# VectorE's 1x1 run in column tiles, the cosine transform on 32x32 tiles, its loads in three slots, and the gathered pixels stored by half steps

## The chip, the cores and the metric

One Trainium2 chip, one core. The metric is device time in microseconds for one launch. Engines are named as in the profile: PE is TensorE's matmul, PEld its weight load, DVE is VectorE, ACT is ScalarE, POOL is GpSimd, SP is SyncE. POOL and SP here mostly issue DMA transfers.

## What is computed

The input x is 8 images of 32 channels and 128 x 128 pixels in float32. Group normalisation is followed by a block matching that picks, for every pixel, the K = 8 best of 25 shifts in a 5 x 5 window and gathers the 32 channels at those shifts, so there are CK = 256 channels. These go two ways, cut here to the lines that matter:

```
xb = _patch_match_stack(x)                     # [8, 256, 128, 128]
dct = _conv(xb, dct_w, groups=C)               # 8 -> 8 channels in each of 32 groups
h = relu(_conv(_conv(xb, w1), w2, groups=CK, pad=1))   # 1x1, then depthwise 3x3
h = relu(_conv(_conv(h, w3), w4, groups=CK, pad=1))
wiener = sigmoid(_conv(_conv(h, w5), w6, groups=CK, pad=1))
filt = _conv(wiener * dct, inv_dct_w, groups=C)
x = x + _conv(filt, agg_w)                     # layer 0
x = x + 5x5 convolution of the normalised x    # layer 1
```

## The kernel before

**Steps and slots.** An image is worked in steps of R = 8 rows, 16 steps and one more that finishes the last rows (NS + 1 = 17 for each image, 136 in all). Each step of the main loop has four slots, in the order i = 3, 2, 1, 0. Slots 3, 2 and 1 each run one of the three pairs "1x1, then depthwise 3x3", each for an earlier step than the one before it in the chain; slot 0 finishes the step that is two behind: it multiplies the sigmoid by the cosine transform and applies the last 1x1. Every slot also gathers one quarter of a step's pixels for the steps to come (`gather_load` three quarters ahead, `gather_select` one ahead, `gather_pixels` now).

**The 1x1 is split over two engines' depthwise convolutions.** `pointwise_t` (matmul line L694, tile p) makes output channels 0 to 127 for a depthwise convolution on PE (`depthwise_t`, L750, tile pw). `pointwise_v` (L670, tile pv) makes output channels 128 to 255 for a depthwise convolution on DVE (`depthwise_v`, L724). `pointwise_t` and `depthwise_t` use weight tiles 32 columns wide, four side by side, each writing 32 partitions of the output. `pointwise_v` uses one weight tile of 128 x 128: for each half step of 4 rows, two matmuls of 512 elements that add up. A float32 matmul shows in the trace as two matmul records.

**The cosine transform.** `gather_pixels` (L632, tile pg) fills xb, which `pointwise_v` and `pointwise_t` read, and which is stored to a DRAM tensor xbd once for each step (L641, one transfer of 1 MB). Since the transform is needed much later than the 1x1, `final_load` loads the 8 rows again from xbd as xf (L790, eight transfers of 128 KB, issued together at the end of slot 0). xf has one buffer. `final_dct` (L809, tile pc) multiplies xf by ldct on four 64 x 64 tiles of the array, two banks of PSUM at a time, and DVE multiplies the result into acc (L817). `final_add` (L830, tile pa) follows in the next slot; DVE adds its result to the input (L838).

**Order.** PE, DVE and ACT run their instructions in the order in which the program writes them. Between these fixed pieces small background tasks are let in from queues: D (DVE, rationed by `tick`), A (ACT), P and Q (PE). They make the next image's costs and the layer 1 of the image before (`layer1`, its matmul is L923 with 64 x 64 tiles, from queue P). POOL's and SP's orders are left to a list scheduler, by program order and readiness. Tiles pv, p, pg, pc, pa and L923's p share a PSUM pool ps_x of five banks. Transfers issued by POOL use eight semaphores in turn, so one waits until the eighth before it has landed.

Of the kernel before, what the change touches and what calls it, by code (L numbers as in the profile page):

```python
# [8 lines left out]
F32 = mybir.dt.float32  # L9
# [6 lines left out]
P = 128  # L16
C, K, H, W = 32, 8, 128, 128
CK = C * K
# [25 lines left out]
def bm3d_conv_preact(  # L44
# [58 lines left out]
    lw5 = const.tile([P, 2, CK], F32, name="lw5")  # L103


    ldct = const.tile([P, 2, 64], F32, name="ldct")
    lagg = const.tile([P, 2, C], F32, name="lagg")


# [90 lines left out]

    queues = {"D": deque(), "A": deque(), "P": deque(), "Q": deque()}

    PAIR = 1.95
    pairs = [0]
# [90 lines left out]

    def mixes():

        dq = work.tile([P, 2, K], F32, name="dq", tag="dq", bufs=1)  # L300
        src = dct_w.rearrange("(m h c i) k a b -> m h k c (i a b)", m=2, h=2, i=K)
        for k in range(K):
            for m in range(2):
                for h in range(2):
                    p = 64 * h + 8 * k
                    nc.sync.dma_start(dq[p : p + 8, m], src[m, (h + m + 1) % 2, k])
        m8 = work.tile([P, 8], F32, name="m8", tag="m16", bufs=1)
        yield "D", 1.0, 10
        nc.vector.tensor_reduce(
            m8,  # L310
            cst[:, C_M32 : C_M32 + C].rearrange("p (a c) -> p c a", c=8),
            axis=mybir.AxisListType.X,
            op=ALU.add,
        )
        for m in range(2):
            nc.vector.tensor_tensor(
                ldct[:, m].rearrange("p (c i) -> p c i", i=K),
                m8.unsqueeze(2).to_broadcast([P, 8, K]),
                dq[:, m].unsqueeze(1).to_broadcast([P, 8, K]),
                ALU.mult,  # L320
            )

        iv = work.tile([P, 2, K], F32, name="iv", tag="iv", bufs=1)
        nc.sync.dma_start(iv, inv_w.rearrange("(m p) k a b -> p m (k a b)", p=P))
        ag = work.tile([C, CK], F32, name="ag", tag="xr")
        nc.sync.dma_start(ag, agg_w.rearrange("c i a b -> c (i a b)"))
        for m in range(2):
            yield "D", 0.5
            ib = work.tile([P, P], F32, name=f"ib_{m}", tag="xm")
            nc.vector.tensor_tensor(  # L330
                ib.rearrange("p (c k) -> p c k", k=K),
                cst[:, C_M16 : C_M16 + 16].unsqueeze(2).to_broadcast([P, 16, K]),
                iv[:, m].unsqueeze(1).to_broadcast([P, 16, K]),
                ALU.mult,
            )
            yield "P", 0
            ps = ps_x.tile([P, 512], F32, name=f"ps_ag_{m}", tag="x")[:, :C]
            nc.tensor.transpose(ps, ag[:, m * P : (m + 1) * P], ident[:C, :C])
            agt = work.tile([P, C], F32, name=f"agt_{m}", tag="agt")
            nc.scalar.copy(agt, ps)  # L340
            yield "P", 0
            ps2 = ps_x.tile([P, 512], F32, name=f"ps_ia_{m}", tag="x")[:, :C]
            nc.tensor.matmul(ps2, ib, agt, start=True, stop=True)
            nc.scalar.copy(lagg[:, m], ps2)
# [276 lines left out]
    def gather_pixels(b, s4, f):  # L621

        n, h = s4 // 2, s4 % 2
        if h == 0 and f == 0:
            xbs[b, n] = xbp.tile([P, 2, R, W], F32, name=f"xb_{b}_{n}", tag="xb")
        xb, xt = xbs[b, n], xts[b, s4]
        sels = [selss.pop((b, s4, f, k2)) for k2 in range(2)]
        pg = ps_x.tile([P, 2, 4, HW], F32, name=f"pg_{b}_{s4}_{f}", tag="x")
        for t in range(NT // 2):
            xa, xz = TW * t, min(TW * (t + 1), HW)  # L630
            for j in range(4):
                nc.tensor.matmul(  # L632
                    pg[C * j : C * (j + 1), :, :, xa:xz],
                    xt[: 8 * QW, f * (NT // 2) + t],
                    sels[j // 2][: 8 * QW, :, j % 2, :, xa:xz],
                    start=True,
                    stop=True,
                )
        nc.scalar.copy(xb[:, :, 4 * h : 4 * h + 4, HW * f : HW * (f + 1)], pg)
        if h == 1 and f == 1:  # L640
            nc.gpsimd.dma_start(xbd[b][:, :, R * n : R * (n + 1)], xb)  # L641

# [15 lines left out]
    def pointwise_v(i, b, n, lhsT, src):  # L660

        v = tv[i - 1]
        if n == NS:
            nc.gpsimd.memset(v[:, i + 1 : 6], 0.0)
        r0, r1 = (i - 1 if n == 0 else 0), (R if n < NS else i - 1)
        for h in range(0, r1, 4):
            hr = min(4, r1 - h)
            ps = ps_x.tile([P, 4, W], F32, name=f"pv{i}_{b}_{n}_{h}", tag="x")
            for g in range(2):
                nc.tensor.matmul(  # L670
                    ps[:, :hr],
                    lhsT[:, g, P:CK],
                    src(g)[:, h : h + hr],
                    start=g == 0,
                    stop=g == 1,
                )
            a = max(h, r0)
            nc.scalar.copy(v[:, 2 + a : 2 + h + hr, 1 : 1 + W], ps[:, a - h : hr])  # L678

# [89 lines left out]
    def final_load(b, n):  # L769
        j0, j1 = (3, R) if n == 0 else (0, R if n < NS else 3)  # L770
        ya, yz = R * n - 3 + j0, R * n - 3 + j1

        whole = j1 - j0 == R
        nr, nw = (2, W) if whole else (j1 - j0, C)
        xr = work.tile([P, 2 * W], F32, name=f"xr_{b}_{n}", tag="xr")
        xr = xr[:, : nr * nw].rearrange("p (r w) -> p r w", w=nw)
        for j in range(4):
            ra = ya + 2 * j if whole else ya
            xa = 0 if whole else C * j
            nc.gpsimd.dma_start(  # L780
                xr[C * j : C * (j + 1)], x[b, :, ra : ra + nr, xa : xa + nw]
            )

        xf = xbp.tile([P, 2, R, W], F32, name=f"xf_{b}_{n}", tag="xf", bufs=1)
        src = xbd[b].rearrange("(j m h c) g y x -> g m h j c y x", j=4, m=2, h=2)
        for m in range(2):
            for h in range(2):
                for g in range(2):
                    p = 64 * h + C * g
                    nc.gpsimd.dma_start(  # L790
                        xf[p : p + C, m, j0:j1], src[g, m, (h + m + 1) % 2, :, :, ya:yz]
                    )
        return xr, xf, j0, j1

    def final_dct(b, n, acc, xf, j0, j1):

        for r0 in range(0, R, 4):
            a, z = max(r0, j0), min(r0 + 4, j1)
            if a >= z:
                continue  # L800


            pc = [
                ps_x.tile([P, 4, W], F32, name=f"pc_{b}_{n}_{m}_{r0}", tag="x") for m in range(2)
            ]
            for h in range(2):
                for m in range(2):
                    o = 64 * ((h + m + 1) % 2)
                    nc.tensor.matmul(  # L809
                        pc[m][o : o + 64, : z - a],  # L810
                        ldct[64 * h : 64 * h + 64, m],
                        xf[64 * h : 64 * h + 64, m, a:z],
                        start=True,
                        stop=True,
                    )
            for m in range(2):
                nc.vector.tensor_mul(acc[m][:, a:z], acc[m][:, a:z], pc[m][:, : z - a])  # L817

    def final_add(b, n, acc, xr, j0, j1):

# [26 lines left out]
    def layer1(b):  # L847
# [60 lines left out]
        for c in range(0, C, 8):  # L908
            if c == 0 or not last:
                yield "D", 2.0, 1 if last else 3  # L910
                normalise(c)
            yield "P", 0
            ps = [
                ps_x.tile([P, 4, W], F32, name=f"p5_{b}_{c}_{e}", tag="x") for e in range(2)
            ]
# [107 lines left out]
    def turn(credit):  # L1023
        now[0] += 1
        run("D", credit)
        run("A")
        run("P")
        run("Q")

    def until(cond, credit):  # L1030
# [3 lines left out]
    with tc.manual_schedule(engines=ORDERED):  # L1034
        push(prep(0))
        push(weights())
        push(mixes())
        xbd[0] = dram.tile([P, 2, H, W], F32, name="xbd_0", tag="xbd")
        for i in range(3):
            nc.gpsimd.memset(tb[i][0:64, :, 0], 0.0)  # L1040
        for u in range(7):
# [12 lines left out]
        for s in range(len(steps) + 2):  # L1054
            if s < len(steps):
                b, n = steps[s]
                if s == 2:
                    push(bands())
                if n == (0 if b else 4) and b + 1 < NB:
                    until(lambda: b in ready, 4.0)  # L1060
                    push(prep(b + 1))
                if n == NS - 1 and b + 1 < NB:
                    until(lambda: b + 1 in ready, 4.0)
                    xbd[b + 1] = dram.tile([P, 2, H, W], F32, name=f"xbd_{b+1}", tag="xbd")
            for i in (3, 2, 1, 0):
                si = s - (i - 1 if i else 2)
                live = 0 <= si < len(steps)
# [15 lines left out]
                run("P")  # L1083
                if live and not i:
                    final_dct(bi, ni, accs[3, bi, ni], xf, j0, j1)

                run("Q")
                if s < len(steps):
# [18 lines left out]
                if live and not i:  # L1107
                    later = end(bi, ni, xr, j0, j1)
                if not i and 0 <= s - 1 < len(steps):
                    fins[s - 1] = final_load(*steps[s - 1])  # L1110
        next(kept, None)
        for _ in later:
            pass
# [63 lines left out]
```

## Time and profile before

| | us |
|---|---|
| median of three runs | 6739.54 |
| lowest, highest | 6728.39, 6740.50 |
| the profiled execution | 6733.76 |
| its span, first to last instruction | 6732.0 |

Busy shares of the span: PE 94%, DVE 87%, ACT 75%, POOL 53%; the mean granted TensorE clock is 0.979. A busy PE is not a PE at its peak: the ends of matmuls are modelled, and overlapping matmuls are merged. How densely PE really works is read from the distance between the starts of consecutive groups of matmuls. In the rows of the timeline, "x8" is the number of records, and the bracket at a line's end is idle time and what ended it.

### The profile page before, as it was taken

Reading aid. Unit: us, or ns where it says so; the run is one execution under the profiler, and the core shown is the slowest. Engines: PE = TensorE matmul, PEld = TensorE weight load, DVE = VectorE, ACT = ScalarE, POOL = GpSimd, SP = SyncE. Lnnn points to the kernel's source line nnn. Section 1 sums busy time; section 2 is a strip of 40 time slices with the busy share of each in tenths; the row PEclk is TensorE's granted clock in tenths of the full one; section 3 lists DMA queues with packets and bytes.
Section 4 is the critical chain, followed back from the end, with each engine's and each line's share of the span. In section 5 each row is a group of like instructions: output and inputs, shape, how many; then the busy total and the mean of one; then the engine's idle time right before and its main releaser. Section 6 shows DMA issues by size and latency. Waiting matters only on the chain. (4 is left out here: it accounts for less than half of the span.)

```text
span 6732.0 us, 216242 instructions
## 1 busy us (share of the span) xinstructions
PE 6334.0 (94%) x92898; PEld 3283.2 (49%) x92898; DVE 5863.1 (87%) x8826; ACT 5060.0 (75%) x6698; POOL 3535.4 (53%) x5527
## 2 busy tenths in 40 slices
PE   5898899999999999999999999999999999999997
PEld 1454455454555545554554545545445454454553
DVE  7889988999889998898988998899888889877776
ACT  5787778777687777877777776877768777687772
POOL 8355447544475454654546544565446654344334
PEclk8899999999999999999999999999999999999998
DMA  4666666766666675666756657566665666566663
GB/s 95 148 151 154 146 153 149 166 154 158 153 158 157 149 166 139 165 155 155 173 129 166 163 144 167 144 167 159 148 155 146 165 151 154 141 164 166 157 150 83
DMA packets 811645, 1020.36 MB, mean 152 GB/s; under 512 B 257072, under 2 KB 622192, under 8 KB 810688
## 3 DMA queue, kind: packets, MB, share of 16 engines
q0 software_dynamic: 424608, 747.17, 44.3%
q1 hardware_dynamic: 383568, 258.11, 17.8%
q8 instruction: 732, 11.99, 0.8%
q10 hardware_dynamic: 2512, 1.25, 0.1%
q14 instruction: 225, 1.84, 0.1%
HBM read 554.82 MB, written 217.54 MB: 115 GB/s over the span
## 5 line engine op out<-in xcount | busy, mean ns | idle before, releaser
L724 DVE SCALAR_TENSOR_TENSOR acc<-tv,dwv,acc 128x1024 f32<-128x1024 f32 (+3 forms) x3264 | 4032.2, 1237 | 256.0 <-ACT acc L721 148.2
L750 PE MATMUL pw<-t,dwd 96*32 96x254 f32 (+7 forms) x31680 | 2127.8, 421 | 74.8 <-DMA t<-t 52.2
L603 POOL DMA_DIRECT2D ib<-idxd x1024 | 749.5, 733 | 1615.0 <-ACT sel L618 1352.0
L750 PEld LDWEIGHTS pw<-t,dwd 96*32 96x32 f32 (+1 forms) x31680 | 1056.9, 111 | 936.0 <-issue 442.8
L617 ACT ACTIVATE ib<-ib,nplace 128x1024 bf16<-128x1024 bf16 x1024 | 1170.6, 1143 | 50.4 <-DMA ib<-idxd 50.4
L618 ACT ACTIVATE sel<-ib 128x1024 f32<-128x1024 bf16 x1024 | 1085.8, 1060 | 32.6
L694 PE MATMUL p<-acc,lw 128*32 128x256 f32 x16768 | 998.3, 383 | 22.8 <-ACT tv L678 22.8
L670 PE MATMUL pv<-acc,lw 128*128 128x512 f32 (+1 forms) x2112 | 970.5, 601 | 29.9 <-DVE acc L817 24.2
L790 POOL DMA_DIRECT2D xf<-xbd x1088 | 650.9, 629 | 282.6 <-DMA out_dram<-xy 82.3
L694 PEld LDWEIGHTS p<-acc,lw 128*32 128x32 f32 x16768 | 558.5, 111 | 454.4 <-ACT tv L678 57.8
L450 ACT ACTIVATE df<-df 128x786 f32<-128x786 f32 (+2 forms) x576 | 467.6, 860 | 331.3 <-DVE df L442 328.6
L678 ACT COPY tv<-pv 128x512 f32<-128x512 f32 (+2 forms) x784 | 436.6, 578 | 370.0 <-PE pv L670 364.6
L632 PE MATMUL pg<-sel,xt 120*32 120x88 f32 (+1 forms) x24576 | 612.7, 244 | 62.1 <-ACT sel L618 46.6
L632 PEld LDWEIGHTS pg<-sel,xt 120*32 120x32 f32 x24576 | 553.1, 111 | 235.1 <-ACT sel L618 60.5
L670 PEld LDWEIGHTS pv<-acc,lw 128*128 128x128 f32 x2112 | 378.9, 191 | 480.6 <-issue 384.3
L442 DVE TENSOR_TENSOR df<-xn 128x786 f32<-128x786 f32 (+2 forms) x576 | 531.8, 974 | 83.3 <-PE pd L457 82.3
L763 ACT ACTIVATE acc<-pw 128x512 f32<-128x512 f32 (+2 forms) x808 | 440.4, 573 | 197.8 <-PE pw L750 195.6
L728 ACT ACTIVATE acc<-acc 128x1024 f32<-128x1024 f32 (+3 forms) x408 | 417.3, 1023 | 225.1 <-DVE acc L724 224.9
L701 ACT COPY t<-p 128x512 f32<-128x512 f32 x800 | 424.2, 570 | 119.0 <-PE p L694 116.9
L721 ACT ACTIVATE acc<-tv,dwv 128x1024 f32<-128x1024 f32 (+3 forms) x408 | 454.8, 1115 | 50.6 <-PE pa L830 33.7
L670 PE MATMUL pv<-xb,lw 128*128 128x512 f32 x1024 | 474.8, 606 | 0.0
L694 PE MATMUL p<-xb,lw 128*32 128x256 f32 x8192 | 467.5, 380 | 0.0
(155 smaller groups left out, 5911.1 us busy)
## 6 DMA issues: line engine op xcount, KB each, us to landing
ib<-idxd POOLq DMA_DIRECT2D x1024, 256.0 KB, 4.7
xbd<-xb POOLq DMA_DIRECT2D x128, 1024.0 KB, 6.9
xf<-xbd POOLq DMA_DIRECT2D x960, 128.0 KB, 7.2
t<-t SPq DMA_DIRECT2D x792, 128.0 KB
t<-t SPq DMA_DIRECT2D x384, 256.0 KB
tv<-tv SPq DMA_DIRECT2D x384, 130.0 KB
xt<-xtd POOLq DMA_DIRECT2D x240, 180.0 KB, 4.7
xtd<-xl POOLq DMA_DIRECT2D x192, 96.0 KB, 3.0
```

The source lines that it names most:

```text
L442: nc.vector.tensor_sub(df[:, :, ca:cz], xn[:, r0 : r0 + SR, ca:cz], xn[:, r0 + dy : r0 + dy + SR, ca + dx : cz + dx],)
L450: nc.scalar.activation(df[:, :, ca:cz], df[:, :, ca:cz], AF.Square)
L603: nc.gpsimd.dma_start(ib.rearrange("p g k y x -> p g (k y x)"), idxd[b][s4 % 8 // 2, s4 // 8 * 2 + s4 % 2, f] .rearrange("(g e k) x -> e g ...
L617: nc.scalar.activation(ib, ib, AF.Square, bias=nplace)
L618: nc.scalar.activation(sel, ib, AF.Relu, scale=-1.0, bias=1.0)
L632: nc.tensor.matmul(pg[C * j : C * (j + 1), :, :, xa:xz], xt[: 8 * QW, f * (NT // 2) + t], sels[j // 2][: 8 * QW, :, j % 2, :, xa:xz], star ...
L670: nc.tensor.matmul(ps[:, :hr], lhsT[:, g, P:CK], src(g)[:, h : h + hr], start=g == 0, stop=g == 1,)
L694: nc.tensor.matmul(ps[C * r : C * (r + 1), e, :nb], lhsT[:, g, s], rows[:, r : r + 4 * nb - 3 : 4], start=g == 0, stop=g == 1,)
L721: nc.scalar.activation(acc, rows, AF.Copy, scale=tap)
L724: nc.vector.scalar_tensor_tensor(acc, rows, tap, acc, op0=ALU.mult, op1=ALU.add)
L750: nc.tensor.matmul(pt[u][C * j : C * (j + 1), ka:kz, :nb, xa:xz], dwd[0:hi, i - 1, u, j, dx + 1], t[0:hi, j, ka:kz, :nb, xa + dx : xz + dx ...
L790: nc.gpsimd.dma_start(xf[p : p + C, m, j0:j1], src[g, m, (h + m + 1) % 2, :, :, ya:yz])
```

## The change

Four parts.

1. `pointwise_v` issues four matmuls of 32 output columns (j = 0 to 3) in place of one of 128. The result and the number of streamed elements for each tile are the same.
2. `final_dct` works on 32 x 32 tiles. For each s of four (which half of the channels, which 4 rows) four tiles on a diagonal of the array write the four quadrants of one PSUM bank: sixteen tiles and four banks in all. ldct, its loads (64 small transfers in place of 32) and xf's channel order are changed to fit.
3. `final_load` becomes a generator that issues the loads of xf in four pieces: s = 0 at the end of slot 0, s = 1 at the end of slot 3, s = 2 and 3 at the end of slot 2. Each piece has one transfer, or two where the partitions wrap around. xbd's layout becomes [256, 128, 128], and the store is made for each half step, in four transfers of 32 partitions.
4. layer 1's matmuls get a queue L of their own, run in slots 3, 2 and 1 and not in slot 0.

```diff
-        if h == 1 and f == 1:
-            nc.gpsimd.dma_start(xbd[b][:, :, R * n : R * (n + 1)], xb)
+        if f == 1:
+            for j in range(4):
+                nc.gpsimd.dma_start(
+                    xbd[b].rearrange("(c g j) y x -> j c g y x", g=2, j=4)[
+                        j, :, :, 4 * s4 : 4 * s4 + 4
+                    ],
+                    xb[C * j : C * (j + 1), :, 4 * h : 4 * h + 4],
+                )
...
             for g in range(2):
-                nc.tensor.matmul(
-                    ps[:, :hr],
-                    lhsT[:, g, P:CK],
-                    src(g)[:, h : h + hr],
-                    start=g == 0,
-                    stop=g == 1,
-                )
+                for j in range(4):
+                    nc.tensor.matmul(
+                        ps[C * j : C * (j + 1), :hr],
+                        lhsT[:, g, P + C * j : P + C * (j + 1)],
+                        src(g)[:, h : h + hr],
+                        start=g == 0,
+                        stop=g == 1,
+                    )
...
-        src = xbd[b].rearrange("(j m h c) g y x -> g m h j c y x", j=4, m=2, h=2)
-        for m in range(2):
-            for h in range(2):
-                for g in range(2):
-                    p = 64 * h + C * g
+        yield xr, xf, j0, j1
+        src = xbd[b].rearrange("(m p) y x -> m p y x", m=2)
+        for s in range(4):
+            if s:
+                yield
+            m, r0 = s // 2, s % 2 * 4
+            a, z = max(r0, j0), min(r0 + 4, j1)
+            for pa, pz, at in ((0, P - C * s, C * s), (P - C * s, P, 0)):
+                if a < z and pa < pz:
                     nc.gpsimd.dma_start(
-                        xf[p : p + C, m, j0:j1], src[g, m, (h + m + 1) % 2, :, :, ya:yz]
+                        xf[pa:pz, m, a:z],
+                        src[m, at : at + pz - pa, R * n - 3 + a : R * n - 3 + z],
                     )
...
+        parts = [(s, max(s % 2 * 4, j0), min(s % 2 * 4 + 4, j1)) for s in range(4)]
+        parts = [(s, a, z) for s, a, z in parts if a < z]
+        pc = {
+            s: ps_x.tile([P, 4, W], F32, name=f"pc_{b}_{n}_{s}", tag="x") for s, a, z in parts
+        }
+        for s, a, z in parts:
+            for q in range(4):
+                o = C * ((q + s) % 4)
+                nc.tensor.matmul(
+                    pc[s][o : o + C, : z - a],
+                    ldct[C * q : C * (q + 1), s],
+                    xf[C * q : C * (q + 1), s // 2, a:z],
+                    start=True,
+                    stop=True,
+                )
+        for s, a, z in parts:
+            m = s // 2
+            nc.vector.tensor_mul(acc[m][:, a:z], acc[m][:, a:z], pc[s][:, : z - a])
...
-            yield "P", 0
+            yield "L", 0
...
                 if live and not i:
                     final_dct(bi, ni, accs[3, bi, ni], xf, j0, j1)
+                else:
+                    run("L")
...
                 if not i and 0 <= s - 1 < len(steps):
-                    fins[s - 1] = final_load(*steps[s - 1])
+                    loads = final_load(*steps[s - 1])
+                    fins[s - 1] = next(loads)
+                if 0 <= s - (1 if not i else 2) < len(steps):
+                    for _ in range({0: 1, 3: 1, 2: 2, 1: 0}[i]):
+                        next(loads)
```

More of the change, by code (lines that the diff above doesn't have):

```diff
@@ L103, in bm3d_conv_preact @@
     lw5 = const.tile([P, 2, CK], F32, name="lw5")
-    ldct = const.tile([P, 2, 64], F32, name="ldct")
+    ldct = const.tile([P, 4, C], F32, name="ldct")
     lagg = const.tile([P, 2, C], F32, name="lagg")
@@ L197, in bm3d_conv_preact @@
     xtd, xbd, idxd, x1d, stats = {}, {}, {}, {}, {}
-    queues = {"D": deque(), "A": deque(), "P": deque(), "Q": deque()}
+    queues = {"D": deque(), "A": deque(), "P": deque(), "L": deque(), "Q": deque()}
     PAIR = 1.95
@@ L298, in mixes @@
     def mixes():
-        dq = work.tile([P, 2, K], F32, name="dq", tag="dq", bufs=1)
-        src = dct_w.rearrange("(m h c i) k a b -> m h k c (i a b)", m=2, h=2, i=K)
-        for k in range(K):
-            for m in range(2):
-                for h in range(2):
-                    p = 64 * h + 8 * k
-                    nc.sync.dma_start(dq[p : p + 8, m], src[m, (h + m + 1) % 2, k])
-        m8 = work.tile([P, 8], F32, name="m8", tag="m16", bufs=1)
+        dq = work.tile([P, 4, K], F32, name="dq", tag="dq", bufs=1)
+        src = dct_w.rearrange("(m q c i) k a b -> m q c k (i a b)", m=2, q=4, i=K)
+        for s in range(4):
+            for q in range(4):
+                for c in range(4):
+                    p = C * q + K * c
+                    nc.sync.dma_start(dq[p : p + K, s], src[s // 2, (q + s) % 4, c])
+        m4 = work.tile([P, 4], F32, name="m4", tag="m16", bufs=1)
         yield "D", 1.0, 10
         nc.vector.tensor_reduce(
-            m8,
-            cst[:, C_M32 : C_M32 + C].rearrange("p (a c) -> p c a", c=8),
+            m4,
+            cst[:, C_M32 : C_M32 + C].rearrange("p (a c) -> p a c", a=4),
             axis=mybir.AxisListType.X,
@@ L314, in mixes @@
         )
-        for m in range(2):
+        for s in range(4):
             nc.vector.tensor_tensor(
-                ldct[:, m].rearrange("p (c i) -> p c i", i=K),
-                m8.unsqueeze(2).to_broadcast([P, 8, K]),
-                dq[:, m].unsqueeze(1).to_broadcast([P, 8, K]),
+                ldct[:, s].rearrange("p (c i) -> p c i", i=K),
+                m4.unsqueeze(2).to_broadcast([P, 4, K]),
+                dq[:, s].unsqueeze(1).to_broadcast([P, 4, K]),
                 ALU.mult,
@@ L784, in final_load @@
         xf = xbp.tile([P, 2, R, W], F32, name=f"xf_{b}_{n}", tag="xf", bufs=1)
-        src = xbd[b].rearrange("(j m h c) g y x -> g m h j c y x", j=4, m=2, h=2)
-        for m in range(2):
-            for h in range(2):
-                for g in range(2):
-                    p = 64 * h + C * g
+        yield xr, xf, j0, j1
+        src = xbd[b].rearrange("(m p) y x -> m p y x", m=2)
+        for s in range(4):
+            if s:
[4 more added lines that the diff above has]
+                if a < z and pa < pz:
@@ L790, in final_load @@
                     nc.gpsimd.dma_start(
-                        xf[p : p + C, m, j0:j1], src[g, m, (h + m + 1) % 2, :, :, ya:yz]
+                        xf[pa:pz, m, a:z],
+                        src[m, at : at + pz - pa, R * n - 3 + a : R * n - 3 + z],
                     )
-        return xr, xf, j0, j1
+        yield
     def final_dct(b, n, acc, xf, j0, j1):
[L797 to L817, printed above, removed]
+        parts = [(s, max(s % 2 * 4, j0), min(s % 2 * 4 + 4, j1)) for s in range(4)]
@@ new lines, in final_dct @@
+        parts = [(s, a, z) for s, a, z in parts if a < z]
[3 more added lines that the diff above has]
+        for s, a, z in parts:
+            for q in range(4):
+                o = C * ((q + s) % 4)
[6 more added lines that the diff above has]
+                )
@@ L1037, in bm3d_conv_preact @@
         push(mixes())
-        xbd[0] = dram.tile([P, 2, H, W], F32, name="xbd_0", tag="xbd")
+        xbd[0] = dram.tile([CK, H, W], F32, name="xbd_0", tag="xbd")
         for i in range(3):
@@ L1063, in bm3d_conv_preact @@
                     until(lambda: b + 1 in ready, 4.0)
-                    xbd[b + 1] = dram.tile([P, 2, H, W], F32, name=f"xbd_{b+1}", tag="xbd")
+                    xbd[b + 1] = dram.tile([CK, H, W], F32, name=f"xbd_{b+1}", tag="xbd")
             for i in (3, 2, 1, 0):
@@ L1085, in bm3d_conv_preact @@
                     final_dct(bi, ni, accs[3, bi, ni], xf, j0, j1)
+                else:
+                    run("L")
                 run("Q")
```

## The prediction

> **What bounds the kernel now.** I read the page first, then the stretches of time, the timeline of PE over one step, and the waits. From the page, the engines and the slices:
>
> ```profile
> PE 6334.0 (94%) x92898; PEld 3283.2 (49%) x92898; DVE 5863.1 (87%) x8826; ACT 5060.0 (75%) x6698; POOL 3535.4 (53%) x5527
> ...
> PE   5898899999999999999999999999999999999997
> ...
> DVE  7889988999889998898988998899888889877776
> ```
>
> PE is nearly full, and DVE is not far behind it: two engines, each with the whole image's chain running through it. The stretches (columns: span, then busy PE, PEld, DVE, ACT, POOL) say where which of them leads:
>
> ```profile
> 4200.00:5000.00 800.00, 767.55 (x11433) 400.82 (x11426) 719.48 (x1089) 623.60 (x826) 435.13 (x679) 0.99 0.65 157
> ...
> 5800.00:6400.00 600.00, 592.63 (x9067) 310.93 (x9056) 471.60 (x488) 456.28 (x588) 266.11 (x423) 1.00 0.63 158
> ```
>
> With the next image's costs in the background (first line) PE is at 96% and DVE at 90%. In the last image, which has no next one (second line), PE is at 99%, DVE at 79%: PE alone sets the pace.
>
> How much of a busy PE is work? In the timeline of PE (start, length, group) the distance between starts is what counts:
>
> ```profile
> 3001.69 3.70 PE L670 MATMUL pv<-xb,lw 128*128 128x512 f32 x8
> 3005.32 0.87 PE L457 MATMUL pd<-df,neg 128*32 128x390 f32 x8
> 3006.00 3.64 PE L694 MATMUL p<-xb,lw 128*32 128x256 f32 x64
> 3009.45 1.13 PE L632 MATMUL pg<-sel,xt 120*32 120x88 f32 x48
> 3010.41 5.31 PE L750 MATMUL pw<-t,dwd 96*32 96x512 f32 x48
> 3015.65 1.95 PE L809 MATMUL pc<-xf,ldct 64*64 64x512 f32 x16
> 3017.52 1.15 PE L632 MATMUL pg<-sel,xt 120*32 120x88 f32 x48
> ...
> 3022.96 2.79 PE L750 MATMUL pw<-t,dwd 96*32 96x256 f32 x48 [1.71 <-DMA t<-t]
> ...
> 3067.91 2.97 PE L809 MATMUL pc<-xf,ldct 64*64 64x512 f32 x16
> 3070.81 1.15 PE L632 MATMUL pg<-sel,xt 120*32 120x88 f32 x48
> ```
>
> p: 64 records in 3.45 us, four side by side, so 16 sets of 256 elements at 0.216 us, or 0.43 us for 512. pv: 8 records of 512 in 3.63 us. The weight loads of pv show its pitch:
>
> ```profile
> 3001.69 0.30 PEld L670 LDWEIGHTS pv<-xb,lw 128*128 128x128 f32 x2 [0.41 <-issue]
> 3002.22 0.19 PEld L670 LDWEIGHTS pv<-xb,lw 128*128 128x128 f32 x1 [0.24 <-issue]
> 3002.65 0.19 PEld L670 LDWEIGHTS pv<-xb,lw 128*128 128x128 f32 x1 [0.24 <-issue]
> ```
>
> Also 0.43 for 512. So one wide tile and four narrow ones stream at the same rate, and the split itself buys nothing. What pv has on top are its ends: the first distance is 0.53 (0.10 too long), and 0.09 pass between the end of its eighth (3001.69 + 0.53 + 7 x 0.43 = 3005.23) and the next group. Reading the single starts in the trace, another 0.11 lie between the end of the pw before it and its own start, and 0.03 in the head of the next group: 0.33 to 0.34 us for going into the 128 x 128 arrangement and back. From pd to p, both 32 columns wide, there is nothing (3005.68 + 0.33 for 390 elements is 3006.00).
>
> **The change part by part.**
>
> *pv.* By the order of the matmuls in the trace PE goes 490 times into a stretch of 128 x 128 work; 314 of these hold pv alone, the others also transposes, which keep their switch. Gain on PE: 314 x 0.338 = 106 us. Streaming is unchanged (8 sets of 0.43); the records go from 8 to 32 a call, and p above issues such records without a gap. Layer 1's matmuls (28 stretches) used to follow pv or precede pc in part and now pay both of their own ends, some 8 us. Net 98.
>
> *pc.* Now 1.87 us: 4 sets x 0.43 = 1.72, and 0.15 of ends. After: 32 records of 512. If all sixteen tiles run together that is 2 sets, 0.86, with the ends as before (32 x 32 is again another arrangement) and about 0.1 for issuing twelve more loads before the first set is complete: 1.1 us, a gain of 0.77. There are 2112 / 16 = 132 full steps' worth: 101 us. This is the disputed term. The trace never runs more than four tiles at once. What it shows is that in pc today four tiles (two row tiles x two column tiles) start within 0.02 us of each other and the next four 0.43 later, although both row tiles write the same bank, in different partitions.
>
> The Trainium skill speaks here on both sides. "TensorEngine Tiling (Array Packing)", section Restrictions and Gotchas, says that different row tiles cannot use one PSUM bank at the same time. The new pc puts four row tiles into each bank, so by that rule its sixteen tiles go one at a time within each bank, on the order written four in a row: 8 sets, 3.43 + 0.15 us, 1.7 us worse than now. The row above contradicts the rule for two row tiles in one bank, so I do not follow it. "TensorE: Matmul & The Clock Gate", Part 3 (Measured speedup vs the span model), gives 10.6 times for sixteen tiles, not 16: an estimate from that is 0.86 x 16 / 10.6 = 1.3 us, a gain of about 0.5 instead of 0.77, 66 us instead of 101. I take the trace's 101 and keep 66 as the lower end of the good case; the bounds outside it are 5 sets (if the second pass of one diagonal holds up the next diagonal; 2.15 us, minus 57 us) and 8 sets (minus 226 us).
>
> *DVE* has the same multiplications (four of 128 x 512 a step): nothing. PSUM: pc takes four of five banks as before. Where layer 1 sat directly before pc, pc took 2.90 in place of 1.87 (the last two timeline lines), since two banks were still held; 13 such places, 13 us, go away, but layer 1 comes up elsewhere, where pv or p want those banks. I count it as zero, within plus or minus 13.
>
> *POOL and DMA.* Stores: 8 transfers of about 0.63 us (the mean of today's 128 KB xf issue) for one of 0.73: +4.3 us a step, 128 steps, +551. Loads: 7 for 8 (3 in the last step of an image): 168 fewer, -106. POOL's busy time goes to about 3980, 59%. It is covered by POOL's longest wait, where it stands before ib loads until ACT is done:
>
> ```profile
> POOL ib L603 <- ACT sel L618: 1352.0, 414, 9.3
> ...
> DVE xr L838 <- PE pa L830: 280.0, 68, 10.6
> ...
> PE pw L750 <- DMA t<-t: 52.2, 32, 4.4
> ```
>
> That is 10 us a step against 3.3 added. If that cover were gone, the price would be at most the 3.3 us, in the steps where POOL is late. Behind a waiting store stand the next ib and xf; ib is asked for two slots ahead. Bytes are the same, in pieces of 2 KB for 4 KB; today's packets of 2048 bytes take 0.09 us and those of 4096 0.19, so the DMA engines see no difference. SP: 32 more tiny transfers of dq at 0.72 us, 23 us, at 24 us into the run; SP's first other work is at 204 us. Zero.
>
> *xf's lead.* Today the last xf issue stands 34 us (median; least 7.5) ahead of pc, and a landing takes:
>
> ```profile
> DMA to landing us min/median/max: 2.5/7.0/14.8
> ```
>
> The pieces s = 2 and 3 are now written one slot (about 12 us) before pc. If POOL also issues them there, behind four stores, about 5 us of lead remain for 7 of landing, and PE waits some 2 us a step. The scheduler may issue them earlier, since they are ready once the last pc is done, and the trace shows POOL transfers issued ahead of earlier ones that wait. I take zero; bounds are 0 and +2 x 132 = 264 us.
>
> *What of PE's 199 us reaches the end.* DVE waits for PE (xr for pa) in 68 of 136 steps, by 4 us each: there PE is late, and 1.5 us saved a step are 1.5 us of time. In the other half DVE arrives after PE, and a shorter PE mostly waits longer. In the last image, 17 steps, all counts. So (17 + 119 / 2) / 136 = 56%, plus part of the rest, since the two are only a few us apart: two thirds. A second loss: slot 0 has neither pv nor p, and in 32 steps its pw waits for a t<-t transfer, which a shorter pc doesn't hasten: included. 199 x 2/3 = 133. From the profiled execution's 6733.8: 6601; the median of the runs shown is 5.8 above it, so 6600 to 6606. I say 6600.
>
> **The rivals.**
>
> *Sixteen tiles don't run together* (slower side). At 8 sets pc costs 3.58 us; PE gets +226 - 98 = +128, and work added to the fuller engine counts nearly whole: about 6850. It decides from the point where pc takes more than 1.87 + 98 / 132 = 2.6 us, between 5 and 6 sets. For it: the rule above, and nothing in the trace shows sixteen. Against it: pc's two row tiles in one bank. At 5 sets the kernel would still gain, about 6705. Chance of 6 sets or more 8%, of about 5 sets 5%.
>
> *xf comes late.* +264 on PE against -199: 6750 to 6800. Chance 8%; halfway, near no change, 3%.
>
> *DVE becomes the bound.* DVE's 5863 us don't shrink, and at 6600 it is at 89% overall and 93% where the next image is prepared. If only the last image's 17 steps and a quarter of the rest gain (25 + 45 us): about 6670. For it: 90% against 96%. Against it: of DVE's idle 869 us, 280 are spent on pa. Chance 14%.
>
> *The main case*, 6600 (6525 to 6650): 62%. The upper limit of the gain is all 199 us and some calmer t<-t transfers because of smaller stores: 6520.
>
> **How the numbers follow.** About 0.2%, 13 us, is what a measurement of this kernel can tell from no change. Faster: 62 + 14 + 5 and a part of the halfway case, 81%; within 0.2%: 3%; slower: 8 + 8 = 16%. The range leaves out the slower cases and the best tail: 6520 to 6720.[...]
>
> **What would show it.** Right: pv appears as 128*32 with 32 records a call, its start-to-next is 3.45 where it was 3.63, and the 0.11 before it is gone; pc reads 32*32, x32, with about 1.1 us to the next group; "issue" waits before pv shrink; DVE's wait for pa falls from 280, its wait share elsewhere rises; POOL is near 59%. Wrong: pc above 2.6 us; a wait of pc on a transfer of xf; PE waiting for DVE or ACT more than 100 us longer than before (then DVE is the bound); new waits for ib in ACT (then POOL is).

## The result and the profile after

The changed kernel is no faster, and by a little slower: 6745.13 us (median of 12 runs, 6736.35 to 6756.93) against 6733.99 us (median of 12, 6725.13 to 6742.49) for the kernel before on the same chip. The ratio is 1.0019, with a 95% interval of 1.001 to 1.0028. The forecast was 6600 us, range 6520 to 6720. The profiled execution of the changed kernel has a span of 6735.4 us (before: 6732.0) and a mean granted TensorE clock of 0.969 (before: 0.979).

The page's line of engines, after:

```profile
PE 6200.2 (92%) x104418; PEld 3213.7 (48%) x104418; DVE 5863.8 (87%) x8828; ACT 5056.7 (75%) x6698; POOL 3845.5 (57%) x6255
```

PE is busy for 134 us less than before, in a span that is no shorter: so much has turned into idle time. The two stretches (span, then busy PE, PEld, DVE, ACT, POOL, then clock, DMA share, GB/s) say the same. In the stretch with the next image's preparation PE went from 96% to 94%:

```profile
4200.00:5000.00 800.00, 748.55 (x12668) 381.94 (x12662) 714.22 (x1084) 617.39 (x818) 470.94 (x765) 0.98 0.62 154
5800.00:6400.00 600.00, 587.40 (x10418) 315.17 (x10414) 478.30 (x494) 463.70 (x600) 302.82 (x507) 0.99 0.62 160
```

Where nothing waits, the two edits of PE's work did what they were to do. The timeline of PE after, for a step like the one shown before:

```profile
2993.07 5.36 PE L757 MATMUL pw<-t,dwd 96*32 96x256 f32 x96
2998.23 3.63 PE L677 MATMUL pv<-xb,lw 128*32 128x512 f32 x32
3001.67 0.85 PE L457 MATMUL pd<-df,neg 128*32 128x393 f32 x8
3002.33 3.64 PE L701 MATMUL p<-xb,lw 128*32 128x256 f32 x64
3005.78 1.15 PE L632 MATMUL pg<-sel,xt 120*32 120x88 f32 x48
3006.72 5.33 PE L757 MATMUL pw<-t,dwd 96*32 96x512 f32 x48
3011.98 1.33 PE L817 MATMUL pc<-xf,ldct 32*32 32x512 f32 x32
3013.24 1.16 PE L632 MATMUL pg<-sel,xt 120*32 120x88 f32 x48
```

From pv's start to the next start it is now 3.44 us, eight sets of 0.43 and nothing else; before, it was 3.63. The weight loads of that pv come in fours, 0.43 apart from the first on:

```profile
2998.23 0.14 PEld L677 LDWEIGHTS pv<-xb,lw 128*32 128x32 f32 x4
2998.66 0.14 PEld L677 LDWEIGHTS pv<-xb,lw 128*32 128x32 f32 x4 [0.29 <-issue]
```

The pw ahead of it takes 5.16 us from start to start, and pd behind it 0.66, without the 0.11 and 0.03 that lay there before. pc takes 1.26 us (3011.98 to 3013.24) where it took 1.87: its 32 records do run as two sets of sixteen tiles. Read singly in the trace, the first sixteen start within 0.29 us and the next sixteen begin 0.45 us after the first, so four row tiles in one bank do not hold each other up.

The time went elsewhere. The waits after (us in total, times, longest): POOL's, DVE's and pw's answer to those shown of before, the others are pc's:

```profile
POOL ib L603 <- ACT sel L618: 1256.4, 406, 13.2
DVE xr L847 <- PE pa L839: 275.2, 66, 13.1
PEld pc L817 <- DVE acc L826: 80.5, 12, 7.2
PE pc L817 <- DVE acc L826: 69.6, 12, 6.2
PE pw L757 <- DMA t<-t: 43.9, 21, 5.2
PE pc L817 <- DMA xf<-xbd: 25.0, 7, 6.4
```

DVE's wait for pa, which the prediction took for PE being late, is 275 us where it was 280. And pc waits in twelve places for DVE's multiplication (L826) to free a PSUM bank, 70 us together. One such place, in PE's timeline and then in DVE's (whose first row is cut at the window's edge):

```profile
2921.62 4.48 PE L932 MATMUL p<-xm,band 64*64 64x512 f32 x40
...
2959.68 1.19 PE L817 MATMUL pc<-xf,ldct 32*32 32x512 f32 x24
2966.58 1.93 PE L817 MATMUL pc<-xf,ldct 32*32 32x512 f32 x8 [5.71 <-DVE acc L826]
```

```profile
2948.92 17.01 DVE L731 SCALAR_TENSOR_TENSOR acc<-tv,dwv,acc 128x1024 f32<-128x1024 f32 x13
2965.85 1.87 DVE L826 TENSOR_TENSOR acc<-acc,pc 128x512 f32<-128x512 f32 x3
2968.58 0.69 DVE L826 TENSOR_TENSOR acc<-acc,pc 128x512 f32<-128x512 f32 x1 [0.86 <-PE pc L817]
2969.18 1.28 DVE L944 TENSOR_TENSOR xy<-xy,p 128x512 f32<-128x512 f32 x2
```

Layer 1's matmul (2921.62) fills two of the five banks; DVE empties them at 2969.18, since the addition L944 comes from the rationed background queue. pc comes in between and finds three banks: 24 of its 32 records run, and the last eight wait until DVE is through with its taps (2965.85). In the kernel before, layer 1 held two banks just as often, for 9 to 24 us, but where it met pc it stood directly ahead of it:

```profile
3063.61 4.48 PE L923 MATMUL p<-xm,band 64*64 64x512 f32 x40
```

```profile
3058.07 10.52 DVE L724 SCALAR_TENSOR_TENSOR acc<-tv,dwv,acc 128x1024 f32<-128x1024 f32 x8
```

So pc came 4.3 us later, at 3067.91, when DVE's taps were nearly through (their end: 3068.59), and was done in 2.90 us. The four pieces of layer 1 in each of images 2 to 7, before, hold their banks for 23, 9, 24 and 9 us from the end of their matmuls; after: 23, 44, 9 and 25.

Such a wait is followed by a second loss. The same place in stretches, the granted clock is the third column from the right:

```profile
2950.00:2959.00 9.00, 9.00 (x157) 4.50 (x160) 8.79 (x8) 8.68 (x12) 1.47 (x2) 1.00 0.72 189
2959.00:2966.00 7.00, 1.87 (x32) 0.28 (x24) 6.82 (x7) 2.88 (x4) 1.42 (x2) 0.89 0.41 119
2966.00:2971.00 5.00, 4.42 (x64) 2.31 (x68) 4.09 (x10) 0.56 (x1) 1.93 (x3) 0.50 0.16 42
2971.00:2976.00 5.00, 5.00 (x96) 2.81 (x92) 4.35 (x22) 2.99 (x5) 5.00 (x4) 0.97 0.36 88
```

After the wait PE runs at half its clock: pg takes 1.71 us from start to start (2968.44 to 2970.15) in place of 0.97. Over the whole run the trace grants half clock for 421 us, before for 288. Of PE's waits behind the first 600 us of the changed kernel's trace, all 28 of 4 us or more have half clock beginning in them or within 4 us of their end, and 18 of the 48 of 2 to 4 us have it too.

### The profile page after: what moved, and what is told of

It is laid out like the page before. It is cut to its first block, busy times and chain, and to the rows that moved or that the text cites. A ratio compares the mean times of both kernels' runs of the same rounds, so it can differ in the third digit from the quotient of the medians.

```text
span 6735.4 us, 240331 instructions
## 1 busy us (share of the span) xinstructions
PE 6200.2 (92%) x104418; PEld 3213.7 (48%) x104418; DVE 5863.8 (87%) x8828; ACT 5056.7 (75%) x6698; POOL 3845.5 (57%) x6255
## 5 line engine op out<-in xcount | busy, mean ns | idle before, releaser
L757 PEld LDWEIGHTS pw<-t,dwd 96*32 96x32 f32 (+1 forms) x31680 | 1082.9, 111 | 916.0 <-issue 423.2
L677 PE MATMUL pv<-acc,lw 128*32 128x512 f32 x8448 | 955.0, 589 | 52.5 <-DVE acc L826 39.6
L642 POOL DMA_DIRECT2D xbd<-xb x1024 | 546.1, 569 | 100.1 <-DMA ib<-idxd 33.6
L801 POOL DMA_DIRECT2D xf<-xbd x920 | 494.7, 551 | 177.0 <-PE pc L817 99.7
L677 PEld LDWEIGHTS pv<-acc,lw 128*32 128x32 f32 x8448 | 282.4, 110 | 539.0 <-issue 417.7
L677 PE MATMUL pv<-xb,lw 128*32 128x512 f32 x4096 | 469.9, 593 | 0.0
```

Source lines behind the costliest of these rows:

```text
L642: nc.gpsimd.dma_start(xbd[b].rearrange("(c g j) y x -> j c g y x", g=2, j=4)[j, :, :, 4 * s4 : 4 * s4 + 4], xb[C * j : C * (j + 1), :, 4 * ...
L677: nc.tensor.matmul(ps[C * j : C * (j + 1), :hr], lhsT[:, g, P + C * j : P + C * (j + 1)], src(g)[:, h : h + hr], start=g == 0, stop=g == 1,)
L757: nc.tensor.matmul(pt[u][C * j : C * (j + 1), ka:kz, :nb, xa:xz], dwd[0:hi, i - 1, u, j, dx + 1], t[0:hi, j, ka:kz, :nb, xa + dx : xz + dx ...
L801: nc.gpsimd.dma_start(xf[pa:pz, m, a:z], src[m, at : at + pz - pa, R * n - 3 + a : R * n - 3 + z],)
```

## The experiments

Four theories were set up in turn. A: layer 1's own queue holds PSUM banks over the next pc. B: PE and DVE take turns, and what PE saves becomes a wait for DVE (or for ACT behind DVE). C: POOL has too much to do, and xf comes late. D: as B, but because the background work of DVE is heaped into slot 0. All ratios are to the kernel before on the same chip.

**Layer 1's queue alone, in the kernel before** (before_L), and the changed kernel without it (after_P), cut to the line that differs:

```diff
-            yield "P", 0        # layer1, in the kernel before
+            yield "L", 0        # and run("L") in slots 3, 2, 1
```

> The kernel before with one part of the change alone: layer 1's matmul in the queue L (slots 3, 2 and 1 only). Theory A (banks): the queue moves this matmul from just before pc to a slot from which its two PSUM banks are held over the next pc until DVE's additions, rationed by tick, come; pc then has three of its four banks and stands until DVE has done its eight taps. Two such places an image of about 8 us and one of 9 in the slot before: 7 x 25 = 175 us at most, so 6800 to 6900. Theory B (DVE is the bound, whatever PE saves): no change, 6725 to 6745. Theory C (POOL and the late xf loads take the gain): no change either.

> The changed kernel with layer 1's matmul back in the queue P; all else as changed. Theory A: the 8 us waits of pc for DVE go away but for the places where this matmul stands directly before pc (about 2 us each, two an image); of PE's 199 us two thirds come through: 6610 to 6660, pc waiting for DVE acc under 50 us in all. Theory B: 6730 to 6750. Theory C: 6730 to 6750, with pc waiting for xf as before.

before_L took 6801.12 us, ratio 1.0102 (1.0082 to 1.0123): the queue alone costs about 69 us. Layer 1's banks are now held for 23, 45, 9 and 25 us, and the waits show the same mark (in the kernel before PE has no such wait, and PEld 11.6 us of it, at most 0.9 at a time):

```profile
PEld pc L809 <- DVE acc L817: 66.3, 12, 5.9
PE pc L809 <- DVE acc L817: 55.8, 12, 5.0
```

after_P took 6693.95 us, ratio 0.9942 (0.9923 to 0.9962): without the queue, the rest of the change gains 0.58%, 39 us. With after_P_late below it has the lowest ratio of the kernels that compute everything, though the intervals of before_pv, after_P_once and after_P_even overlap with its own. So A is right about part 4, worth 52 us inside the change (1.0019 - 0.9942 = 0.77%), but falls short of its 6610 to 6660: most of the expected gain is lost in another way.

**Layer 1's additions let in earlier, changed kernel** (after_add). The queue L stays; the addition is taken out of DVE's ration and run in the same slot.

```diff
-            yield "D", 3.6 if last else 1.6
+            if last:
+                yield "D", 3.6
+            else:
+                yield "A", 0
```

> The changed kernel with one edit: DVE's two additions after layer 1's matmul are run in the same slot (queue A) and not when tick's ration allows. The queue L stays. Theory A: both banks are free before the next pc, so the waits of pc for DVE fall to the level of the kernel before and the gain appears: 6590 to 6650. Theory B: 6730 to 6750, since DVE has the same work. Theory C: 6730 to 6750.

It took 6752.44 us, 1.0035 (1.0022 to 1.0049): a miss. The banks come free earlier (held for 9, 15, 16 and 15 us), but the addition now stands in DVE's fixed order behind the taps, and pv is what waits for it:

```profile
PEld pv L677 <- DVE xy L947: 77.9, 15, 8.4
PE pv L677 <- DVE xy L947: 69.2, 14, 8.2
```

**pv's column tiles alone, in the kernel before** (before_pv), the diff's second hunk and nothing else:

> The kernel before with pv in column tiles alone. PE loses 314 switches of 0.338 us, 106 us. Theory A: two thirds of it, 6655 to 6680. Theory B: no change, 6725 to 6745. Theory C: as A, since no transfer is changed.

6694.72 us, 0.9951 (0.9933 to 0.9969): 33 us come out of about 98 that PE saves.

**All pieces of xf at once, at the end of slot 0** (after_P_once, otherwise after_P), and **the store once for each step** (after_P_store1: after_P with four transfers of 256 KB in place of eight of 128 KB):

```diff
-                if 0 <= s - (1 if not i else 2) < len(steps):
-                    for _ in range({0: 1, 3: 1, 2: 2, 1: 0}[i]):
+                    for _ in range(4):
                         next(loads)
```

> The changed kernel with layer 1's matmul in queue P, and all pieces of xf issued at the end of slot 0 again. Once an image, where POOL issues 31 transfers of the next image's xtd in a row, the last piece of xf is now issued 3 us after pc has started (before: 9 us ahead), and pc with the column set after it loses some 8 us. Theory C (late xf): this goes away, 7 x 6 to 8 us less than with the three slots: 0.9942 falls to 0.986 to 0.988 of the kernel before, 6635 to 6650. Theory B (DVE takes up what PE saves): no more than 10 us less, 6680 to 6695, with PE's wait moved on to pv.

> The changed kernel with layer 1's matmul in queue P, and the gathered pixels stored once a step (four transfers of 256 KB) and not by half steps (eight of 128 KB). POOL loses 512 issues of 0.57 us, 290 us of its time. Theory C in the form 'POOL's load costs time': 20 to 40 us less than 6694. Theories A and B: no difference beyond 10 us, since POOL's added work lies in its wait for ACT.

In after_P (33.0 us in all), as in the changed kernel (25.0), a piece of xf comes late for pc about once an image, where POOL is busy with a row of some 30 other transfers (L422). In the changed kernel:

```profile
2804.60 1.09 PE L817 MATMUL pc<-xf,ldct 32*32 32x512 f32 x16
2809.85 4.15 PE L817 MATMUL pc<-xf,ldct 32*32 32x512 f32 x16 [4.16 <-DMA xf<-xbd]
```

after_P_once has no such wait left, and took 6703.91 us, 0.9947 (0.9929 to 0.9964), as much as after_P: C is out as the cause. PE waits in other places instead. One of them is pv, for a bank that DVE's multiplication of pc frees; in the kernel before that wait is 24.2 us. Another is pw, for the transfers t<-t, 52.2 us in the kernel before; whether these come late because of DVE was not followed:

```profile
PE pv L677 <- DVE acc L826: 55.7, 28, 3.2
PE pw L757 <- DMA t<-t: 78.9, 31, 6.4
```

after_P_store1 took 6727.45 us, 0.999 (0.9978 to 1.0001), 0.5% slower than after_P: the half-step stores help, by some 32 us. With one store, xf (which reads what was stored) is late by more, 47.5 us against after_P's 33.0; where the rest of the 32 us lies was not traced:

```profile
PE pc L817 <- DMA xf<-xbd: 47.5, 7, 10.0
```

**DVE lighter by one tap of eight** in its depthwise convolutions (before_tap, after_P_once_tap), which leaves out a ninth of the convolution's sum and takes 495 us from DVE, nothing from PE:

```diff
-            ((1, 1), (0, 0), (0, 1), (0, 2), (1, 0), (1, 2), (2, 0), (2, 1), (2, 2))
+            ((1, 1), (0, 0), (0, 1), (0, 2), (1, 0), (1, 2), (2, 0), (2, 1))
```

> The kernel before, with the last of DVE's eight multiply-add taps left out of the depthwise convolution (part of the computation is not done; the time is what is asked): DVE loses 384 x 1.28 = 493 us. If PE alone bounds the kernel before: 6700 to 6730. If PE and DVE take turns in bounding it (theory B): 100 to 200 us less, 6530 to 6630. It is the pair of the next run.

> The kernel of the run after_P_once, with the same tap left out (part of the computation is not done). Theory B: with DVE unloaded PE's saving comes through nearly whole, so this is 130 to 200 us below before_tap, a larger difference than the 35 to 95 between after_P_once and the kernel before. If DVE isn't the reason, the two differences are the same within 15 us.

before_tap: 6596.42 us, 0.9788 (0.9767 to 0.9808). after_P_once_tap: 6503.5 us, 0.9657 (0.9639 to 0.9675). Taking work from DVE alone gains 137 us in a kernel whose PE was 94% busy, so PE alone did not set the pace. And with DVE lighter, the same edits on PE gain 93 us instead of 30: B, though under the 130 to 200 that it expected.

**The ration of DVE's background work moved out of slot 0** (D), in after_P and, as a control, in the kernel before (the end of one line; the comment is added here):

```diff
-    * (0.4 if i == 0 else 0.2)
+    * (0.25 if i == 0 else 0.25)     # _even;  _late: 0.1 and 0.3
```

> The changed kernel with layer 1 in queue P, and the ration of DVE's background work spread evenly: a quarter of a step's ration in each slot, where slot 0 had 0.4 and the others 0.2. Theory D (what PE saves in slot 0 is lost again because ACT's activation of acc stands in ACT's order behind df, and df waits for DVE, whose background work is heaped into slot 0): with less of it in slot 0 the wait of PE in slot 3's pv (151 us in the sum for the kernel with layer 1 in P) falls under 110 and the time to about 6620 to 6660, at least 30 us more gain than the same edit brings to the kernel before. Rival B' (DVE's sum of work is what counts, wherever it stands): time within 15 us of 6694, the wait turns up in other slots.

> As the even split, but only a tenth in slot 0 and 0.3 in each other slot. D: slot 3's pv wait is lowest here, under 80 us, the time 6600 to 6660, unless the taps of the other slots are now held up in the same way. B': within 15 us of 6694 or slower.

> Control: the kernel before with the even split. D: the wait in slot 3's pv is 101 us there and PE's slot 0 is longer, so less to gain: 6705 to 6735. If it gains as much as the changed kernel does, the split was simply not the best for either, and D doesn't explain where the change's gain went.

> Control: the kernel before with a tenth in slot 0. D: 6700 to 6750, less gain than the changed kernel has with the same edit.

after_P_even: 6707.03 us, 0.9959 (0.9944 to 0.9974). after_P_late: 6690.46 us, 0.9934 (0.9915 to 0.9953). before_even: 6747.2 us, 1.0018 (1.0009 to 1.0028). before_late: 6746.02 us, 1.0014 (1.0 to 1.0029). The even split costs both kernels some 12 us; the late one is 4 us better in after_P and 11 worse in before (in after_P both differences lie inside the intervals), and neither comes near the 6600 to 6660 of D. The wait that D named is the excess of the time from slot 0's pw to slot 3's pv over what PE streams there; it is 147 us in after_P, 181 in _even and 101 in _late, and what _late takes away there comes back between pc and pd (72 to 128 us). D is out: moving DVE's work about moves the waits about. It is the sum that counts.

**Two taps out, and the cosine transform's part alone.** before_tap2 and after_P_once_tap2 leave out another tap (2, 1); before_pc is after_P_once with pv as one matmul of 128 columns again, that is part 2 and part 3's layout and stores, without part 1 (the "4's store" of the expectation is part 3's).

> The kernel before without the last two of DVE's eight taps in the depthwise convolution (about 987 us less work for DVE, the sum is incomplete). With one tap out it took 137 us less than before. Theory B (PE and DVE take turns, and what one saves is a wait for the other): DVE is now far from the bound, so the second tap brings much less than the first, 20 to 70 us: 6525 to 6580. If DVE's chain alone set the time, the second tap would bring as much as the first: about 6460.

> The changed kernel with layer 1 in queue P and all pieces of xf at the end of slot 0, without the last two of DVE's taps (the sum is incomplete). PE has about 175 us less to do than in the kernel before without them. Theory B: the gap to that kernel opens as DVE gets lighter, from some 27 us with all taps and 93 us with one out to 115 to 165 us with two out. Rival E (what PE saves is lost on PE itself, by the granted clock or by unshown costs of the small tiles, whatever DVE does): the gap stays under 100 us.

> The changed kernel with layer 1 in queue P, all pieces of xf at the end of slot 0, and pv again as one matmul of 128 columns: parts 2 and 4's store alone, so to say, against before. PE saves about 80 us. Theory B: the first 98 us (pv alone) brought 33 us, and both together with the pieces at once 27 to 30, so this alone brings 0 to 30 us: 6700 to 6735. If the small tiles bring what the sum of the prediction took (two thirds of 80): about 6680.

before_tap2: 6542.39 us, 0.9706 (0.969 to 0.9722); after_P_once_tap2: 6413.77 us, 0.9519 (0.9503 to 0.9534); before_pc: 6728.96 us, 0.999 (0.9979 to 1.0). The second tap brings the kernel before 54 us, less than the first's 137, and the gap to the changed one opens to 129 us. The pages of the two kernels, before_tap2 and then after_P_once_tap2:

```profile
PE 6267.2 (96%) x92898; PEld 3264.6 (50%) x92898; DVE 4878.2 (75%) x8010; ACT 5075.2 (78%) x6698; POOL 3539.0 (54%) x5527
```

```profile
PE 6115.6 (95%) x104418; PEld 3231.0 (50%) x104418; DVE 4879.1 (76%) x8012; ACT 5054.9 (79%) x6698; POOL 3844.8 (60%) x6255
```

Here PE's busy time falls by 152 us and its share by 0.6 points only (95.8% to 95.2%), since the span falls too. With all taps the same edits, in after_P_once, took PE from 94.1% to 92.7% and moved the time by 30 us. Rival E (the saving is lost on PE itself, whatever DVE does) expected a gap under 100 us and is out as the whole account. In the waits of before_tap2 DVE now waits for PE at pc, for 254.6 us, where in the kernel before it is 42.3 us:

```profile
DVE xr L838 <- PE pa L830: 449.1, 87, 10.4
DVE acc L724 <- ACT acc L721: 365.4, 220, 9.4
DVE acc L817 <- PE pc L809: 254.6, 115, 10.1
```

**By images.** From the first matmul of pc in one image to that in the next, from the traces, us (the last column: the last image, which prepares no other, to its own last pc):

| taps out | kernel | images 2 to 7, mean | last image |
|---|---|---|---|
| none | before, after_P_once | 813.6, 813.0 | 660.9, 647.5 |
| one | before_tap, after_P_once_tap | 795.8, 782.6 | 661.1, 647.6 |
| two | before_tap2, after_P_once_tap2 | 788.0, 770.7 | 662.0, 646.5 |

In the last image DVE has slack: its work makes no difference (660.9, 661.1, 662.0), and 13 to 15 us of PE's saving come through. That is not all of it: 44 of pv's 314 stretches and 16 of pc's steps lie there, about 24 us (an estimate from 0.33 and 0.61 us each). In before_pc this image takes 650.8 us, so pc's 10 us come through whole; in before_pv it takes 660.4, so of pv's 15 almost nothing does. There PE's idle time grows from 12 to 19 us, mostly in pw's wait for t<-t, and the time at half clock from 6 to 22. So a part of the saving is lost even where DVE is not in the way. In the images that prepare the next one, the same saving is worth 0.6 us with all taps, 13 with one out, 17 with two out.

**Where the saving went.** PE's work is less by 0.33 us for each of pv's stretches (98 us, as the prediction had it) and by 0.61 us for each pc (132 x 0.61 = 80 us). Against that, in the profiled executions: PE's idle time, summed over all rows of its waits, and the time at half clock, each with its growth against the kernel with as many taps before.

| kernel | PE's work less by | span less by | missing | idle more | half clock more | idle + half of that |
|---|---|---|---|---|---|---|
| before_pv | 98 | 36 | 62 | 46 | 27 | 59 |
| before_pc | 80 | 22 | 58 | 32 | 19 | 41 |
| after_P_once | 178 | 26 | 152 | 91 | 99 | 141 |
| after | 178 | -3 | 181 | 130 | 133 | 196 |
| after_P_once_tap | 178 | 102 | 76 | 70 | 4 | 72 |
| after_P_once_tap2 | 178 | 118 | 60 | 35 | 31 | 51 |

The last column is an estimate: a stretch at half clock is taken to lose half its length, as if PE worked through all of it. The Trainium skill reckons in the same way ("TensorE: Matmul & The Clock Gate", section Terms: the penalty is the throttled time times what the clock lacks). It comes near what is missing in most rows (in before_pc 41 of 58): longer waits, and work at half clock, which was seen to follow such waits. This says where the missing time lies and not why; the cause rests on the runs with taps left out. How much the half clock costs by itself was not tried.

## Why the prediction was wrong

- **What bounds the kernel.** "... there PE is late, and 1.5 us saved a step are 1.5 us of time": the step that failed first. I took DVE's 280 us of waiting for pa as proof that PE was behind. PE and DVE feed each other in a ring (pc to DVE's product, to PE's last 1x1, to DVE's addition; pv to ACT to DVE's taps to ACT to PE again), so each waits for the other somewhere, and a wait on one engine does not say that the other one is the bound. With 178 us taken off PE this wait was 281 us in after_P_once.
- **"What of PE's 199 us reaches the end": two thirds, it said.** Measured without part 4: 30 to 40 us of 178, about a fifth. For pv alone it is a third, for pc's part with the stores a tenth (8 of 80, interval 0 to 14). With one of DVE's taps gone it is half (93 of 178), and only with two gone over two thirds (129). The lines were there: DVE at 90% in the stretch where PE was at 96%. "In the last image ... all counts" failed too, in part: with PE at 99% and DVE at 79% about six tenths came through, 13 to 15 of some 24 us.
- **"Layer 1 comes up elsewhere ... I count it as zero, within plus or minus 13".** It costs 52 us in the change and 69 alone, and this is what turns a small gain into none. I asked which bank would be missing for whom and not how long it is held: the matmul moved away from the one place in which pc came late enough not to mind.
- **pv.** Right: all of the 0.33 us a stretch is gone.
- **pc.** The mechanism is right, sixteen tiles run together, and following the trace's two row tiles in one bank rather than the rule of the Trainium skill, "TensorEngine Tiling (Array Packing)", section Restrictions and Gotchas, was right. The size was off: 1.26 us instead of 1.1, 80 us instead of 101, since 0.29 us pass from the first to the sixteenth start, where I had 0.1; the estimate from the Trainium skill, "TensorE: Matmul & The Clock Gate", Part 3, 1.3 us, was the better one.
- **POOL.** 3845 us instead of 3980 (a store's issue takes 0.57 us and one of xf's loads 0.55, not 0.63). Its added work was hidden: after_P_store1, with 512 stores fewer, is slower. **xf's lead**: seven waits, 25 us, not zero, but without effect on the time (after_P_once). **DVE's own work**: unchanged, as said.
- **The rivals.** "DVE becomes the bound" at 6670 was nearest to the change without part 4 (6694), and it had 14%. Its sign, PE waiting for DVE or ACT over 100 us longer, came true in the changed kernel (285 to 405 us), but with part 4's waits in it; in after_P, without them, it is 317. The rival that ended on the slower side was none of those: a PSUM bank held over one more slot, on top of DVE's bound. That the clock falls after longer waits was not in any sum.

## What to carry over

When two engines are busy for 94% and 87% and depend on each other within each step, expect from one engine only the gain that the other's slack lets through, and find it by stages: here the stage with DVE at 90% let 0.6 of some 22 us an image through, and the last image, with DVE at 79%, 13 of some 24. A wait of B for A does not show that A is the bound; taking a known amount of work from each in turn does. When a PSUM user is moved to another slot, write down when its bank is emptied, and by which queue, and what comes in between.

## What the runs showed of the hardware

- Sixteen 32x32 float32 tiles with four row tiles writing one PSUM bank run together: 32 records of 512 elements in 1.26 us from start to next start, ends included.
- In the changed kernel all of PE's 28 later waits of 4 us or more, and 18 of 48 shorter ones of 2 to 4 us, were followed by stretches of 3.4 us or a few times that at a granted clock of 0.5; over the run such stretches grew from 288 us to 421.
- Two 128 KB stores, one of them issued half a step earlier, beat one of 256 KB by 0.5% here, although POOL issues more; PE's waits for the loads that read them back were 33 us against 47.5.
